# One pool of PSUM banks, a root on GpSimd, and other homes for VectorE's work in a two-layer kernel

## The chip, the cores and the metric

The kernel runs on one core of a Trainium2 chip. The metric is device time in microseconds (us), the median of several executions; one further execution was profiled. In the profile PE is TensorE, PEld its weight loads, DVE is VectorE, ACT is ScalarE, POOL is GpSimd and SP is SyncE, which issues most DMAs.

## The reference

Sixteen sequences of 512 tokens, each token 128 float32 values, go through two layers. Cut to what matters:

```python
# layer 0
xn = layernorm(x)
q, k, v = heads(xn @ Wq.T), heads(xn @ Wk.T), heads(xn @ Wv.T)     # 16 heads of 8
q, k = elu(rope(q)) + 1, elu(rope(k)) + 1
attn = causal linear attention (running sums of k v^T and of k, divided)
p = softmax(xn @ router.T); the best 2 of 8 experts per token, weights normalised
ffn = sum over the 2 experts of weight * relu(xn @ fc[e].T)**2 @ proj[e].T
      + relu(xn @ shared_fc.T)**2 @ shared_proj.T
x = x + attn @ Wo.T + ffn
# layer 1
xn = layernorm(x)
q, k, v = heads(xn @ W_qkv.T)
for each chunk of 64 queries: probs = softmax(q k^T / sqrt(8)) over the keys up to the chunk's end
    a gate from the sums of probs (two steps of a small dynamical system), rescale, probs @ v
xk = mu_k * xn + (1 - mu_k) * xn_previous;  xr likewise with mu_r
mix = sigmoid(xr @ W_r.T) * (relu(xk @ W_k.T)**2 @ W_v.T)
x = x + attn @ W_out.T + mix
```

## The kernel before

The work goes by sequence. A sequence's 512 tokens are four tiles (`NT`) of 128 partitions. Sequences are gathered in groups (`GROUPS`), since the experts need tokens of many sequences at once. For each group there are four chains of work. `dispatch` normalises the sequences (`layernorm_T`), finds the router's logits, routes (`route`, `places`) and scatters every token's row to two slots of a table in memory, by indirect DMAs on the POOL queue (`send`). `slot_tiles` runs over the table in tiles of 128 slots: it loads a tile's rows, turns them (`columns`), loads the weights of the tile's expert, and computes `hidden` (a product `hg_ps`, a rectifier on ACT, a square on DVE or POOL) and `project` (`yg_ps`). `layer0` runs the linear attention (`linear_operands`, `linear_attention`) and the `shared_expert`, whose last product `y` also takes in the attention's output. `layer1` runs, for each sequence, `head` (which gathers expert rows back by indirect DMAs and weighs them in `combine`, normalises, `channel_mix`, `values`, `projected`, `operands`), then `weighted` for each of two halves u of the heads, and then `tail` with `gated` and `gate_factor`.

A group with n token tiles needs a table of 2n + 7 slot tiles (`slot_count`), because each of eight experts may leave a tile part full.

Layer 1's attention works in two passes. `operands` builds padded queries `qa` and keys `ka`, multiplies them into scores (`sc`) and takes each row's maximum on DVE (`maxima`); after a transpose (`mx`) the maximum is taken off `qa`. `weighted` multiplies again with keys on the partitions (`st`), takes the exponential on ACT (`ex`), and multiplies by the padded values (`o`). Score products use 32 rows of the array at a time, products with values 32 columns, all others the full array: three forms of matmul. The linear attention has the same shape: scores with masked queries `q0m`, a causal product `am` on DVE, then `o`.

The order of instructions on each engine is not the order in which the code calls them. The class `Program` collects every operation with its needs and an assumed cost (`COSTS`, `TURN` for a change of matmul form, `HANDOVER` between engines), plays the program through in those costs, and emits each engine's instructions in the order found (`run`, `_take`, `_emit`); each engine then runs its queue strictly in that order. Hence almost every instruction of the profile carries one line (L261), that of the helper. Operations called inside `program.unit()` stay together. Indirect DMAs are kept at least `SPACE` apart in the plan, each placed behind a PE instruction.

The accumulators live in the eight PSUM banks. Two pools share them: `ps_big`, three tiles of two banks, and `ps_one`, two tiles of one bank.

```python
ps_big = pool("ps_big", 3, 24, space=bass.MemoryType.PSUM)
ps_one = pool("ps_one", 2, 24, space=bass.MemoryType.PSUM)
```

A tile comes free when its last reader (DVE or ACT) is done; a score unit of layer 1 asks for two tiles of `ps_big` at once.

Of the kernel before, what the change touches and what calls it, by code (L numbers as in the profile page):

```python
# [36 lines left out]
P = 128  # L37
# [9 lines left out]
GROUPS = (3, 4, 4, 3, 2)  # L47
FIRST = [sum(GROUPS[:g]) for g in range(len(GROUPS))]
GT = max(GROUPS) * NT
QUAD = 4  # L50

# [108 lines left out]
class Base:  # L160


    def __init__(self, slots, make):
        self.slots, self.make, self.tile = slots, make, None
        self.writers, self.readers = [], []
        self.left, self.free_at, self.users = 0, 0.0, []
# [7 lines left out]
class Slots:  # L174
# [3 lines left out]
    def __init__(self, n, ahead):  # L178
        self.free, self.asked, self.taken, self.waiting = [0.0] * n, [], 0, []
        self.ahead = ahead  # L180
# [19 lines left out]

class Op:
# [15 lines left out]
    ("ACT", None): (200, 0.8), ("POOL", None): (120, 1.75), ("SP", None): (80, 0.0),  # L217
}

# [7 lines left out]
class Program:  # L227
# [21 lines left out]
    def call(self, name, api, method, args, kw):  # L249
# [26 lines left out]
        else:  # L276
            form = method if (name, method) in COSTS else None
            if name == "DVE" and method in ("tensor_scalar", "tensor_scalar_min", "tensor_scalar_max"):
                form = "fast"
            if method in ("tensor_reduce", "bn_stats"):  # L280
                n = math.prod(args[1].shape[1:])
            least, each = COSTS[name, form]
            cost = least + each * n
            if kw.get("func", args[2] if len(args) > 2 else None) == AF.Sqrt:
                cost += 2600.0
# [46 lines left out]
    def run(self):  # L332
# [20 lines left out]
        while emitted < len(self.ops):  # L353
# [46 lines left out]
            for base in op.bases:  # L400
                base.left -= 1
                base.free_at = max(base.free_at, end + op.later)
                if not base.left:
                    heapq.heappush(base.slots.free, base.free_at + HANDOVER)
# [9 lines left out]
    def _take(self, op, start, offer):  # L414
# [6 lines left out]
        for bs in by_slots.values():  # L421
            slots = bs[0].slots
            if len(slots.free) < len(bs):
# [7 lines left out]
            ready = max(ready, heapq.nsmallest(len(bs), slots.free)[-1])  # L431
# [3 lines left out]
        for bs in by_slots.values():  # L435
            slots = bs[0].slots
            for b in bs:
                heapq.heappop(slots.free)
# [8 lines left out]
    def _passes(self, new):  # L447
# [9 lines left out]
        for bs in also.values():  # L457
            slots = next(iter(bs)).slots
            if len(slots.free) < len(bs):
# [29 lines left out]
def two_layers(ctx: ExitStack, tc: tile.TileContext, x, small, const, w_fc, w_proj, out):  # L489
# [19 lines left out]
    ps_big = pool("ps_big", 3, 24, space=bass.MemoryType.PSUM)  # L509
    ps_one = pool("ps_one", 2, 24, space=bass.MemoryType.PSUM)  # L510

    def big(name):
        return ps_big.tile([P, 2, 512], F32, tag="big", name=name)

    def one(name):
        return ps_one.tile([P, 512], F32, tag="one", name=name)
# [87 lines left out]
    eps = fixed.tile([P, 1], F32, tag="eps", name="eps")  # L604
    V.memset(eps, LN_EPS)
# [43 lines left out]
    def layernorm_T(xs, xT, name, tag, bufs):  # L649
# [7 lines left out]
        S.activation(rstd, mv[:, :, 1], AF.Sqrt, bias=eps, scale=1.0)  # L657
        V.reciprocal(rstd, rstd)
        xn = p2.tile([P, NT, D], F32, tag=tag, name=f"xn_{name}", bufs=bufs)
        for t in range(NT):  # L660
            V.tensor_scalar(
# [1047 lines left out]
```

## Time and profile before

| what | value |
|---|---|
| runs | 1669.26, 1670.35, 1676.13 us (median 1670.35) |
| profiled execution, its own time | 1665.29 us |
| its span, first to last instruction | 1663.5 us |
| mean granted TensorE clock | 0.973 |
| instructions | 36439 |
| DMA | 167.03 MB, mean 100 GB/s |
| matmul passes `hg_ps`, `yg_ps` | 1304 each, 182.5 and 188.5 us busy |
| `maxima` on DVE | 448 reductions, 385.8 us |
| `ex` on ACT | 320 exponentials, 313.1 us |

A float32 matmul is two passes, so a line of the profile counts two for one call. Busy shares are averages over a program whose stretches differ; the windows of the trace give them by stretch. A wait is booked to what ended it. A matmul that waits inside a row of its like is booked as busy, so the starts of consecutive rows tell more than the busy share. A row of the groups gives operation, output and inputs, shapes, count, busy time, mean length, and then the idle time before it with what ended it.

### The profile page before, as it was taken

What the parts mean: (1) busy time and instruction counts of PE and PEld (TensorE: products, weight loads), DVE (VectorE), ACT (ScalarE), POOL (GpSimd) and SP (SyncE); (2) the same over time, 40 slices, a digit from 0 to 9 for tenths busy, and PEclk for the clock granted to TensorE, in tenths of its full rate; (3) what the DMA queues carried; (4) which work ended last, traced back from release to release, by engine and by line L of the source; (5) the groups of instructions that cost most, each with busy time, mean ns of one, the idle gap of its engine ahead of it and who ended that gap; (6) DMA issues with size and microseconds to landing.
All of it is one profiled execution on the core that took longest, in us unless ns stands there. A gap on an engine that the chain in (4) does not pass through costs nothing.

```text
span 1663.5 us, 36439 instructions
## 1 busy us (share of the span) xinstructions
PE 1547.3 (93%) x14439; PEld 1021.8 (61%) x14439; DVE 1207.5 (73%) x2474; ACT 778.2 (47%) x1191; POOL 539.1 (32%) x485
## 2 busy tenths in 40 slices
PE   4889799999999999999999989999999999999996
PEld 3578776666766566566666656666565656565443
DVE  7875268877578874976758796968786858786773
ACT  4343334545445634444544655454545444535444
POOL 1415255075125421453033603242136202135020
PEclk8899999999999999999999999999999999999998
DMA  5367777144334423243322243324133313110000
GB/s 155 106 211 233 219 218 212 49 141 118 96 107 127 127 87 96 72 121 97 90 90 79 78 122 96 96 63 124 35 94 92 110 33 86 30 51 23 20 1 14
DMA packets 154986, 167.03 MB, mean 100 GB/s; under 512 B 13248, under 2 KB 100672, under 8 KB 154816
## 3 DMA queue, kind: packets, MB, share of 16 engines
q1 hardware_dynamic: 146624, 147.91, 29.9%
q0 software_dynamic: 8192, 16.79, 3.3%
q8 instruction: 114, 1.87, 0.5%
q14 instruction: 56, 0.46, 0.1%
HBM read 122.83 MB, written 41.81 MB: 99 GB/s over the span
## 4 chain that ended last, share of the span: by engine, by line
PE 53%; DVE 10%; issue 5%; ACT 3%; POOL 1%; DMA 0%; SPq 0%; POOLq 0%; ACTq 0%; DVEq 0%
PE o L261 10%; PE sc L261 10%; PE st L261 8%; PE yg_ps L261 5%; PE hg_ps L261 5%; DVE maxima L261 4%; PE y L261 3%; PE h_ps L261 2%; PE qkv L261 1%; PE qk L261 1%; PE ho_a L261 1%; ACT ex L261 1%; PE oh_a L261 1%; PE mx L261 1%; PE cm_r L261 1%
## 5 line engine op out<-in xcount | busy, mean ns | idle before, releaser
L261 DVE TENSOR_REDUCE maxima<-sc 128x2 f32<-128x768 f32 (+2 forms) x448 | 385.8, 912 | 84.6 <-PE sc L261 83.0
L261 ACT ACTIVATE ex<-st 128x1024 f32<-128x1024 f32 x320 | 313.1, 1025 | 177.5 <-PE st L261 176.3
L261 PE MATMUL st<-qa,ka 32*128 32x384 f32 (+3 forms) x2048 | 213.4, 471 | 9.6 <-DVE maxima L261 5.9
L261 PE MATMUL sc<-ka,qa 32*128 32x512 f32 (+2 forms) x1792 | 213.8, 511 | 3.7 <-DVE maxima L261 1.0
L1095 POOL DMA_INDIRECT rows<-xn,pl_slot x128 | 135.1, 1055 | 225.6 <-PE y L261 64.2
L261 PE MATMUL yg_ps<-wp,hg 128*128 128x128 f32 x1304 | 188.5, 287 | 17.5 <-DVE hg L261 9.4
L261 PEld LDWEIGHTS yg_ps<-wp,hg 128*128 128x128 f32 x1304 | 162.6, 195 | 66.9 <-issue 36.6
L1114 POOL DMA_INDIRECT back<-results,pl_slot x128 | 128.4, 1003 | 222.7 <-PE st L261 38.4
L261 PE MATMUL hg_ps<-xgT,wf 128*128 128x128 f32 x1304 | 182.5, 285 | 10.8 <-issue 6.3
L261 DVE TENSOR_TENSOR am<-sc,const_sb 128x1024 f32<-128x1024 f32 x128 | 151.3, 1218 | 53.7 <-PE sc L261 49.2
L261 PEld LDWEIGHTS hg_ps<-xgT,wf 128*128 128x128 f32 x1304 | 163.5, 196 | 35.9 <-issue 23.8
L261 PE MATMUL o<-ex,vpad 128*32 128x512 f32 (+3 forms) x2048 | 175.1, 447 | 1.7 <-ACT yg L261 1.3
L261 PEld LDWEIGHTS st<-qa,ka 32*128 32x128 f32 x2048 | 104.0, 186 | 81.4 <-issue 26.4
L261 ACT ACTIVATE hg<-hg_ps 128x1024 f32<-128x1024 f32 x84 | 84.2, 1002 | 135.7 <-PE hg_ps L261 135.3
L261 POOL TENSOR_TENSOR hg<-hg 128x1024 f32<-128x1024 f32 x34 | 64.6, 1901 | 224.1 <-ACT hg L261 223.9
L261 PEld LDWEIGHTS sc<-ka,qa 32*128 32x128 f32 x1792 | 90.5, 185 | 70.5 <-issue 25.8
L261 PEld LDWEIGHTS o<-ex,vpad 128*32 128x32 f32 x2048 | 52.2, 110 | 83.8 <-issue 59.5
L261 DVE TENSOR_TENSOR hg<-hg 128x1024 f32<-128x1024 f32 (+1 forms) x50 | 62.0, 1241 | 56.4 <-ACT hg L261 56.4
L261 ACT COPY oTs<-o 128x256 f32<-128x256 f32 (+1 forms) x96 | 42.7, 445 | 120.2 <-PE o L261 119.5
L261 ACT COPY yg<-yg_ps 128x256 f32<-128x256 f32 x84 | 30.9, 368 | 131.6 <-PE yg_ps L261 108.6
L261 PE MATMUL o<-am,vpad 128*32 128x128 f32 x2048 | 81.8, 281 | 8.7 <-DVE am L261 8.0
L261 PE MATMUL sc<-q0m,k0T 32*128 32x256 f32 x1024 | 81.3, 410 | 1.6 <-ACT ex L261 1.0
(193 smaller groups left out, 2289.1 us busy)
## 6 DMA issues: line engine op xcount, KB each, us to landing
wf<-in_w_fc SPq DMA_DIRECT2D x163, 256.0 KB
wp<-in_w_proj SPq DMA_DIRECT2D x163, 256.0 KB
results<-yg SPq DMA_DIRECT2D x79, 128.0 KB
xg<-rows SPq DMA_DIRECT2D x37, 256.0 KB
rows<-zeros SPq DMA_DIRECT2D x2, 2496.0 KB
x_in<-in_x SPq DMA_DIRECT2D x16, 256.0 KB
x<-x SPq DMA_DIRECT2D x16, 256.0 KB
out<-rr SPq DMA_DIRECT2D x16, 256.0 KB
```

The lines of the kernel that those rows point to most:

```text
L261: return getattr(api, method)(*map(made, args), **{k: made(a) for k, a in kw.items()})
L1095: i = nc.gpsimd.indirect_dma_start(out=rows.made()[:, :], out_offset=bass.IndirectOffsetOnAxis(ap=slot.made(), axis=0), in_=row.made(), in ...
L1114: "POOL", lambda: nc.gpsimd.indirect_dma_start(out=o.made(), out_offset=None, in_=results.made()[:, :], in_offset=bass.IndirectOffsetOnAxi ...
```

## The change

It has five parts.

1. Groups of 4, 4, 4 and 4 sequences in place of 3, 4, 4, 3 and 2. `LATE` is the first sequence of the last group.
2. One PSUM tile of eight banks. `Banks.place` chooses, for each operation that needs accumulators, which banks it takes (one, or two neighbours), and prefers not to leave single banks. The shared expert's and the experts' hidden products, and the two transposes of the linear attention, take one bank each and are emptied bank by bank.
3. No square root on ACT: the normaliser's root is a power on POOL, so ACT stays with one table of functions.
4. Work of DVE goes elsewhere: squares to ACT, most of `gate_factor` and the weighted sums of `combine` to POOL, the first step of `xr` and `xk` to ACT; for the last four sequences also the normalisation of layer 1, the operands of the first half and the gate's product to POOL. The masked queries `q0m` go from ACT to POOL.
5. The planner's costs for POOL and for DVE's per-partition scalars are new, its look-ahead over PSUM tiles is 48 instead of 24, and the expert products, the projection `yg_ps`, `y` and `qk` are units.

The diff, cut to its core:

```diff
-GROUPS = (3, 4, 4, 3, 2)
+GROUPS = (4, 4, 4, 4)
+LATE = B - GROUPS[-1]
...
+class Banks:
+    def __init__(self, pool, n, ahead):
+        self.pool, self.n, self.whole = pool, n, None
+        self.slots = Slots(n, ahead)
+        self.slots.free = [(0.0, k) for k in range(n)]
...
+    @staticmethod
+    def place(slots, bs, start):
+        free = {k: max(t, start) for t, k in slots.free}
+        best = None
+        def alone(k, rest):
+            return (k ^ 1) in rest
+        def fit(i, rest, at, ready, odd):
+            nonlocal best
+            if i == len(bs):
+                if best is None or ready + 400.0 * odd < best[0][0] + 400.0 * best[0][1]:
+                    best = ((ready, odd), list(at))
+                return
...
-    ("ACT", None): (200, 0.8), ("POOL", None): (120, 1.75), ("SP", None): (80, 0.0),
+    ("ACT", None): (200, 0.8), ("POOL", None): (240, 1.63), ("POOL", "fast"): (120, 1.14),
+    ("POOL", "each"): (60, 2.97), ("POOL", "memset"): (100, 0.84), ("SP", None): (80, 0.0),
...
-    ps_big = pool("ps_big", 3, 24, space=bass.MemoryType.PSUM)
-    ps_one = pool("ps_one", 2, 24, space=bass.MemoryType.PSUM)
+    banks = Banks(
+        ctx.enter_context(tc.tile_pool(name="psum", bufs=1, space=bass.MemoryType.PSUM)), 8, 48
+    )
...
-        S.activation(rstd, mv[:, :, 1], AF.Sqrt, bias=eps, scale=1.0)
-        V.reciprocal(rstd, rstd)
+        G.tensor_scalar_add(rstd, mv[:, :, 1], LN_EPS)
+        G.tensor_tensor(rstd, rstd, root, ALU.pow)
...
-            V.tensor_scalar(
+            (G if late else V).tensor_scalar(
                 xn[:, t, :], xs[:, t, :], mv[:, t, 0:1], rstd[:, t : t + 1], ALU.subtract, ALU.mult
...
-            for o in range(2):
-                r = 2 * u + o
-                S.activation(qm[:, o, :], pts[:, 0, :], AF.Copy, scale=c_("pick")[:, r : r + 1])
+            G.tensor_tensor(
+                qm, qT.unsqueeze(1).to_broadcast([P, 2, T]),
+                c_("pick")[:, 2 * u : 2 * u + 2].unsqueeze(2).to_broadcast([P, 2, T]), ALU.mult,
+            )
...
-            S.activation(hf, ph, AF.Relu)
-            (V if fp or b < GROUPS[0] else G).tensor_tensor(hf, hf, hf, ALU.mult)
+                ph = one(f"h_ps_{b}_{f}")
+                M.matmul(ph, wfc_s[:, f * P : (f + 1) * P], xnT, start=True, stop=True)
+                S.activation(hf[:, i, :], ph, AF.Relu)
+            if fp or b < GROUPS[0]:
+                S.activation(hf, hf, AF.Square)
+            else:
+                G.tensor_tensor(hf, hf, hf, ALU.mult)
...
-            ph = big(f"hg_ps_{g}_{q}_{pair}")
+                ph = one(f"hg_ps_{g}_{q}_{i}")
+                with program.unit():
...
+                S.activation(h[:, ii, :], ph, AF.Relu)
...
-            (V if pair or g == 0 else G).tensor_tensor(o, o, o, ALU.mult)
+            if pair or g == 0:
+                S.activation(o, o, AF.Square)
+            else:
+                G.tensor_tensor(o, o, o, ALU.mult)
...
-            for t in range(NT):
-                n = k * NT + t
-                V.scalar_tensor_tensor(
-                    x1[:, t, :], y[:, t, :], shares[j][:, n, :], x1[:, t, :],
-                    ALU.mult, ALU.add,
-                )
+            share = shares[j][:, k * NT : (k + 1) * NT, :]
+            G.tensor_tensor(y, y, share.to_broadcast([P, NT, D]), ALU.mult)
+            G.tensor_tensor(x1, x1, y, ALU.add)
...
+        A = G
...
-        V.tensor_mul(en, sums, rl)
-        V.tensor_scalar_max(sc, en, 1e-6)
+        A.tensor_mul(en, sums, rl)
+        A.tensor_scalar_max(sc, en, 1e-6)
...
+        if u == 0 and b < LATE:
+            V.scalar_tensor_tensor(
+                halves(qa), halves(q), own, spread("aug_q", u, 1), ALU.mult, ALU.add
+            )
...
+        else:
+            G.tensor_tensor(qa, q, own.to_broadcast([P, T]), ALU.mult)
+            G.tensor_tensor(halves(qa), halves(qa), spread("aug_q", u, 1), ALU.add)
...
-        V.tensor_tensor(ov, ov, fac.unsqueeze(2).to_broadcast([P, NT * H, DH]), ALU.mult)
+        (G if b >= LATE else V).tensor_tensor(ov, ov, fac.unsqueeze(2).to_broadcast([P, NT * H, DH]), ALU.mult)
...
-            V.tensor_scalar_mul(m, xp[:, 0:T], om)
+            S.activation(m, xp[:, 0:T], AF.Copy, scale=om)
```

In `gate_factor` the three reciprocals and the two `scalar_tensor_tensor` stay on DVE and the two tanh on ACT; all else is on POOL.

## The prediction

> **What bounds the kernel now.** I read the page first: busy shares, the slices, then the chain.
>
> ```profile
> PE 1547.3 (93%) x14439; PEld 1021.8 (61%) x14439; DVE 1207.5 (73%) x2474; ACT 778.2 (47%) x1191; POOL 539.1 (32%) x485
> ...
> PE   4889799999999999999999989999999999999996
> ...
> PEclk8899999999999999999999999999999999999998
> ...
> PE 53%; DVE 10%; issue 5%; ACT 3%; POOL 1%; DMA 0%; SPq 0%; POOLq 0%; ACTq 0%; DVEq 0%
> ```
>
> PE is the bound: 93% busy, and 53% of the chain that ended last. But the chain also gives DVE 10% (166 us), so a busy PE is not always a working PE. The timeline of PE shows it: start, length, form.
>
> ```profile
> 648.06 1.06 PE L261 MATMUL hg_ps<-xgT,wf 128*128 128x128 f32 x8
> 648.96 1.08 PE L261 MATMUL cm_k<-xk,small_sb 128*128 128x512 f32 x2
> ...
> 655.41 1.16 PE L261 MATMUL v<-small_sb,xp 128*128 128x128 f32 x8
> 656.49 1.07 PE L261 MATMUL o<-ex,vpad 128*32 128x384 f32 x16
> ...
> 1535.36 1.15 PE L261 MATMUL sc<-ka,qa 32*128 32x384 f32 x16
> 1536.43 1.09 PE L261 MATMUL ho_a<-const_sb,oTs 128*128 128x128 f32 x8
> 1537.46 6.30 PE L261 MATMUL sc<-ka,qa 32*128 32x384 f32 x32
> ```
>
> From start to start, eight expert passes behind their like take 0.90 us, eight passes of that form behind a 32-row stretch 1.08 (655.41 to 656.49), sixteen score passes 1.07. The 32 score passes at 1537.46 should take 2.15 us and are booked busy for 6.30: PE waited for banks that VectorE had not emptied (one `maxima` reduction of 1024 columns is 1.218 us). Spacing every matmul of the program as the undisturbed stretches do (0.22 us for a 128-wide product of full form, 0.11 for a transpose, 0.06 to 0.22 for a 32-row or 32-column one, plus 0.14 to 0.2 for a switch of form) gives an estimate of 1415 us of work in the 1663.5 us span. About 250 us are stalls, start-up, end and clock. The windows say where:
>
> ```profile
> 0.00:60.00 60.00, 33.54 (x210) 21.65 (x210) 45.64 (x163) 23.64 (x46) 14.86 (x31) 0.83 0.47 144
> 60.00:300.00 240.00, 216.18 (x1967) 175.74 (x1971) 158.06 (x352) 97.05 (x163) 101.36 (x90) 0.96 0.66 202
> 300.00:900.00 600.00, 579.75 (x5568) 388.32 (x5567) 446.91 (x875) 288.49 (x451) 202.98 (x175) 0.99 0.34 100
> 900.00:1500.00 600.00, 574.70 (x5452) 363.56 (x5448) 456.58 (x874) 293.43 (x437) 186.24 (x163) 0.99 0.27 79
> ...
> 1527.00:1646.00 119.00, 111.95 (x955) 54.59 (x953) 76.95 (x152) 54.94 (x70) 21.37 (x18) 0.96 0.03 10
> ...
> 1646.00:1663.50 17.50, 4.15 (x19) 3.24 (x19) 7.94 (x29) 1.94 (x5) 0.00 (x0) 0.62 0.05 15
> ```
>
> The first number after the length is PE busy, the third DVE, the fourth ACT, the fifth POOL. PE idles 26 us in the first 60; in the middle DVE is at 75%, POOL at 32%; the last 17.5 us are a chain of small gate operations with PE almost empty.
>
> **The change part by part.** My sum runs against the profiled execution, 1665.3 us; the median of the runs is 1670.35, 5 us above.
>
> *Seven tiles fewer.* A group of n token tiles reserves 2n+7 expert tiles: 163 over five groups, 156 over four. By the groups' rows a tile costs PE (182.5 + 188.5 + 27.1)/163 = 2.44 us: 17 us, all on PE.
>
> *Switches.* `program.unit()` keeps the passes of an expert tile, a projection or the shared output together. In the order of PE's instructions the changes of form fall from 1016 to 943: 73 x 0.15 = 11 us, less about 2 counted with the tiles: 9.
>
> With the same spacing the new program is 1389 us of PE work: 26 less, the same two terms.
>
> *Where the regions lie.* The last `y` product, after which PE has layer 1 alone, stands 65 us of work before the end in the old order and 145 us in the new, because the last group has four sequences, not two. In the trace it ends at 1562: 1350 us of work in 1562 (86%), then 62 in 84 (74%) up to 1646, then the 17.5 us end. At unchanged rates the new program takes 1244/0.864 = 1440, 141/0.74 = 190 and the end. So the long tail takes back about 14 us of the 26.
>
> *The end.* The gate moves 20 of its 25 instructions per sequence from DVE (7.9 us from first reciprocal to last product) to POOL. No row has POOL at 64 columns; from 1.07 us at 512 and 1.90 at 1024 a straight line gives 0.34, with DVE's 0.22 as the lower end and 0.7 (the 512-wide scalar form) as the upper. I take 0.34, since both rows lie on the line: with the hops between engines about 12 us, +4 (0 to +9). End 21.5. Subtotal: 1440 + 190 + 21.5 = 1651.
>
> *DVE relief.* Removed, by group rows: squares 62.0 + 23.0, weighted sums 45.1, gate 80.1, the first halves of `xr`,`xk` 17.1, the root's reciprocal 5.4, a quarter of `qa`,`ka` (39.1), of `xn` (27.2) and of `o1n` (11.1), 19: 252 us, leaving 955 (57 to 58%). One pool of banks also lets a one-bank product take any free bank, where two were set apart before, and the halves of an expert pair are emptied bank by bank. So DVE's part of the stalls should shrink. At unchanged rates 196 us of non-work lie before the tail and 49 in it; I take a fifth off the first (36: start-up and clock stay) and a quarter off the second (13: each late sequence has some 11 us less on DVE). 1651 - 49 = 1602. Bounds: nothing, and a half (-123).
>
> *Root tables.*
>
> ```profile
> L261 ACT ACT_TABLE_LOAD x48 | 61.6, 1283 | 21.2 <-PE st L261 19.2 <-PEq L1699 0.7 <-DVE phi L261 0.6
> ```
>
> One load is left of 48. The row prices one at 1.283 us, 60 in all; the Trainium skill, "ScalarE: Activation LUTs", What ACT_TABLE_LOAD costs, says about 2.7, which would make it 127. The row decides. Either way it is ACT's time and ACT is 47% busy: freed are 61.6 + 9.6 (roots) + 39.4 (`q0m`), and squares (about 70), split rectifiers (15) and `xr`,`xk` (20) come in, so ACT stays near 773 us. What hides it is ACT's slack; on the path only start-up (five loads in its first 30 us) shows it: a few us, inside the fifth above. POOL's power of four columns has no row; between 0.1 (a one-column memset) and 1.9 us (a 1024-wide product), I take 0.3, on the small side.
>
> *POOL.* It gains `q0m` (32 x 1.90 = 61), sums (64 x 1.07 = 68), gate (320 x 0.28 = 90), roots 13 and late parts 11; the operands cost 119 for 128 and ten squares less about -9: 539 becomes about 764, 46%. Each sum also holds the queue for its gather, about 1.7 us (gather issue ends 216.9, first use 218.5), 32 times: 54 us behind which gate and operands stand. Here a rule speaks against the change:
>
> ```profile
> L261 DVE SCALAR_TENSOR_TENSOR x<-back,rt_m,x x128: 318/344/2306, 218.5 to 1572.4; 128x128 f32<-128x128 f32 x128
> ...
> 572.70 2.33 DVE L261 TENSOR_SCALAR xn<-x,ln_mv,ln_rstd 128x128 f32<-128x128 f32 x2
> 573.03 1.92 POOL L261 TENSOR_TENSOR hg<-hg 128x1024 f32<-128x1024 f32 x1 [10.69 <-ACT hg L261]
> ```
>
> The same operation takes 344 ns in the median and 2306 at worst; the second pair shows why: `xn` ends as POOL's product ends. On average (404 ns by its group) this costs 17%, with POOL's tensor work at 16% of the span. That work rises to 29%: 30% of the 215 us of such DVE work that is left, about +30 us. The Trainium skill, "SBUF — State Buffer", Who interferes with whom, calls the shared port pair an exclusive lock, so the loser waits the whole instruction: some 550 such instructions x 29% x 0.5 us = 80. DVE ends at 985 or at 1035, both under 1207: the sum stands by the first, the range keeps the second.
>
> *Edits at nothing.* The causal product in another view, two routing tiles in others' storage, the two transposes in a bank each: same work, same engines. A unit makes others wait for its length (4.66 us for the 40 passes of `y`), but `y` stood nearly whole already (86 stretches, 64 now); if that cover is gone, 16 waits of a few us on ACT, not on PE. The planner's new prices and deeper look-ahead take no time; they reorder all, which is why the fifth above may be a half or nothing.
>
> *DMA and SP.* Seven tiles fewer are 14 weight loads of 256 KB; PE waited 3.2 us for weights in all: nothing, and if that cover is gone, still a gain.
>
> Sum 1602 on the profiled execution; 1607 with the 5 us, rounded to 1608.
>
> **The rivals.**
> *R1, only the arithmetic.* DVE relief frees no bank sooner because the order was already packed to these costs: 1651, 1656 measured. For it: PE shows only 50 us idle between 300 and 1600. Against it: the 6.30 us row, whose waits count as busy.
> *R2, DVE queues behind POOL (slower).* Four DVE instructions of each gate (reciprocals, `gf_z`, `gf_v`) and 28 normalisations now wait for POOL: about 100 waits, each ahead of `maxima` reductions in DVE's queue, which free PE's banks. POOL's queue itself waits for gathers and for the PE instruction behind which each gather is put. Before, DVE's waits of this sort (root from ACT) were 9.7 us over 32, 0.3 each: 30 us, hidden. It decides above 1656 + 100 x d = 1670, 0.15 us a wait that reaches PE with R1's relief, or 0.6 us with mine. At 1 us each with half the relief: 1632 + 100 = 1732, 1700 at 0.7.
> *R3, the stalls were mostly banks.* Half go: 1528 to 1560.
>
> **How the numbers follow.** Mine (1575 to 1645) 0.52, R1 (1645 to 1665) 0.16, R2 (over 1665) 0.18, R3 (under 1575) 0.14. About 0.5%, 8 us, can be told from no change, so faster is below 1662: 0.52 + 0.14 + most of R1 (0.12) = 0.78; same (1662 to 1679) 0.07; slower 0.15. The range 1550 to 1685 leaves a few in a hundred of R3 and a tenth of R2 outside.
>
> **What would show it.** Expert passes 1248 per group instead of 1304; DVE near 985 us, POOL near 764, ACT near 775 with one table load; DVE's share of the chain under 8%; score groups of 32 passes shorter than 6 us in the tail; last 20 us a POOL chain. If DVE's waits for POOL total over 60 us and PE's for DVE do not fall, R2 is right. If DVE is lighter and PE's start-to-start times stay, R1.

## The result, and the profile after

The kernel after takes 1749.05 us (median of four runs, 1741.76 to 1751.2), beside 1672.71 for the kernel before on the same chip. The ratio is 1.0449, with a 95% interval of 1.0408 to 1.0489: slower by about 75 us, where I had forecast 1608 us and a gain. The profiled execution took 1751.2 us, its span 1749.4.

The page of the kernel after: busy times, slices of PE, granted clock by slice, and the shares of the chain that ended last.

```profile
PE 1529.1 (87%) x14316; PEld 1008.2 (58%) x14316; DVE 995.6 (57%) x1803; ACT 774.0 (44%) x1247; POOL 807.3 (46%) x964
...
PE   5788988779899998999999989889998988878885
...
PEclk7789999899999999999999999999999989989898
...
PE 59%; POOL 14%; DVE 11%; issue 7%; DMA 5%; ACT 4%; POOLq 0%; SPq 0%; DVEq 0%; ACTq 0%
```

PE is 18 us less busy than before, in the direction that fewer tiles and fewer changes of form had promised; DVE is 212 us lighter. Yet PE idles 220 us, where it idled 116. In the chain POOL rose from 1% to 14% and DMA from nothing to 5%, although POOL is busy only 46% of the time: its busy share alone does not show this.

The windows of the kernel after, cut where its own stages lie: length, busy time of PE, PEld, DVE, ACT and POOL, then granted clock, DMA share and GB/s. The experts' products run from 136 to 1407 us, the last `y` product ends near 1527.

```profile
60.00:300.00 240.00, 210.55 (x2045) 173.77 (x2044) 97.61 (x213) 99.04 (x183) 90.03 (x84) 0.95 0.60 179
300.00:900.00 600.00, 542.68 (x5134) 361.63 (x5135) 383.15 (x727) 275.98 (x448) 311.93 (x353) 0.96 0.35 105
900.00:1400.00 500.00, 466.49 (x4512) 307.69 (x4513) 287.57 (x428) 234.95 (x379) 200.61 (x239) 0.97 0.28 83
1400.00:1527.00 127.00, 107.58 (x946) 63.69 (x947) 79.86 (x122) 49.31 (x77) 85.75 (x97) 0.91 0.08 24
1527.00:1749.40 222.40, 170.17 (x1596) 82.72 (x1592) 104.80 (x154) 97.55 (x125) 96.30 (x153) 0.89 0.04 11
```

Between 300 and 900 us PE is at 90%, where it was at 97%, with POOL at 52% for 34% and DVE at 64% for 74%. In the last 222 us PE is at 77%. The two kernels do not do the same work in the same stretch, since their groups differ; pool_undone below has this kernel's groups and shows where the time was lost.

The waits of the kernel after, all engines: who waited, for whose output; then us in total, times, and the longest.

```profile
POOL back L317 <- DMA back<-results,pl_slot: 59.5, 29, 4.6
...
DVE gf_z L317 <- POOL gf_z L317: 44.1, 19, 5.4
DVE ln_st L317 <- POOL x L317: 43.6, 11, 9.9
...
PE banks L317 <- DVE maxima L317: 38.2, 42, 4.1
...
DVE xn L317 <- POOL ln_rstd L317: 31.2, 13, 5.1
...
DVE gf_cur L317 <- POOL gf_sc L317: 20.8, 11, 7.2
...
DVE o1n L317 <- POOL gf_rl L317: 14.2, 9, 3.9
...
PE banks L317 <- POOL o1n L317: 11.3, 1, 11.3
...
DVE gf_v L317 <- POOL gf_z L317: 10.4, 11, 2.1
```

DVE's waits for POOL (these, and 1.9 us for `rr`) are 75 waits and 166 us, 2.2 us each. In the kernel before there were three, 8 us in all:

```profile
DVE rr L261 <- POOL hg L261: 6.7, 1, 6.7
DVE rr L261 <- POOL xp L261: 1.1, 1, 1.1
DVE rr L261 <- POOL rr L261: 0.3, 1, 0.3
```

Summed over all its waits, PE's idle time behind DVE rose from 74 to 117 us, behind ACT from 22 to 55, behind POOL from 0.5 to 37. Together that is 113 us more, of which 7 came back in its other waits. The idle time as a whole rose by 104 us; less the 18 by which PE is less busy, it is the 86 us by which the span grew.

The timeline of the kernel after shows what one such wait does: start, length, engine, operation, and in brackets the idle time before it with what ended it.

```profile
301.38 0.94 POOL L1193 DMA_INDIRECT back<-results,pl_slot  x1 [0.31 <-issue]
...
303.59 0.85 PE L317 MATMUL banks<-am,vpad 128*32 128x128 f32 x20
304.93 1.04 POOL L317 TENSOR_TENSOR back<-back,rt_m 128x512 f32<-128x512 f32 x1 [2.61 <-DMA back<-results,pl_slot]
306.05 1.26 POOL L317 TENSOR_TENSOR x<-x,back 128x512 f32<-128x512 f32 x1
307.34 0.29 DVE L317 BATCH_NORM_STATS2 ln_st<-x 128x6 f32<-128x128 f32 x1 [6.71 <-POOL x L317]
...
311.14 2.69 DVE L317 TENSOR_SCALAR xn<-x,ln_mv,ln_rstd 128x128 f32<-128x128 f32 x4 [0.36 <-POOL ln_rstd L317]
...
313.21 1.15 PE L317 MATMUL banks<-const_sb,xn 128*128 128x128 f32 x4 [8.78 <-DVE xn L317]
314.16 1.92 PE L317 MATMUL banks<-xgT,wf 128*128 128x128 f32 x8
...
318.06 0.94 POOL L1193 DMA_INDIRECT back<-results,pl_slot  x1 [2.49 <-PE banks L317]
...
320.68 1.03 POOL L317 TENSOR_TENSOR back<-back,rt_m 128x512 f32<-128x512 f32 x1 [1.68 <-DMA back<-results,pl_slot]
...
321.99 1.04 POOL L317 TENSOR_TENSOR ln_rstd<-ln_rstd,root 128x4 f32<-128x4 f32 x1
...
323.07 1.30 DVE L317 TENSOR_SCALAR xn<-x_in,ln_mv,ln_rstd 128x128 f32<-128x128 f32 x1 [5.07 <-POOL ln_rstd L317]
```

Follow it downwards. POOL issues a gather and then stands 2.61 us for its rows, because the sum is next in its queue. Product and sum take 2.3 us. DVE has the statistics of `x` next in its own queue and stands 6.71 us. PE has the transposes of the normalised rows next and stands 8.78 us: the wait reaches every engine, and each adds its own step to it. Some ten microseconds later the second kind appears. A root for another sequence (`x_in`, layer 0, nothing to do with the gather) lies in POOL's queue behind the gather, the wait for its rows and the product, and DVE stands 5.07 us for four numbers per partition.

### The profile page after: what moved, and what is told of

The parts are those of the page before. It is cut to its first block, busy times and chain, and to the rows that moved or that the text cites. A ratio compares the mean times of both kernels' runs of the same rounds, so it can differ in the third digit from the quotient of the medians.

```text
span 1749.4 us, 36128 instructions
## 1 busy us (share of the span) xinstructions
PE 1529.1 (87%) x14316; PEld 1008.2 (58%) x14316; DVE 995.6 (57%) x1803; ACT 774.0 (44%) x1247; POOL 807.3 (46%) x964
## 4 chain that ended last, share of the span: by engine, by line
PE 59%; POOL 14%; DVE 11%; issue 7%; DMA 5%; ACT 4%; POOLq 0%; SPq 0%; DVEq 0%; ACTq 0%
PE banks L317 59%; DMA back<-results,pl_slot 4%; DVE maxima L317 3%; POOL back L1193 3%; ACT ex L317 1%; POOL q0m L317 1%; POOL back L317 1%; POOL ka L317 1%; POOL ln_rstd L317 1%; POOL x L317 1%; DVE xn L317 1%; POOL hg L317 1%; DVE am L317 1%; ACT hg L317 1%; POOL gf_z L317 1%
## 5 line engine op out<-in xcount | busy, mean ns | idle before, releaser
L317 DVE TENSOR_REDUCE maxima<-banks 128x2 f32<-128x768 f32 (+2 forms) x448 | 384.7, 911 | 136.8 <-PE banks L317 123.1
L317 ACT ACTIVATE ex<-banks 128x1024 f32<-128x1024 f32 x320 | 310.8, 1022 | 157.6 <-PE banks L317 151.8
L317 PE MATMUL banks<-ka,qa 32*128 32x512 f32 (+2 forms) x1792 | 197.7, 526 | 44.6 <-DVE maxima L317 20.1
L317 DVE TENSOR_TENSOR am<-banks,const_sb 128x1024 f32<-128x1024 f32 x128 | 150.7, 1217 | 143.2 <-PE banks L317 133.2
L317 PE MATMUL banks<-qa,ka 32*128 32x512 f32 (+3 forms) x2048 | 197.2, 471 | 25.0 <-DVE maxima L317 12.6
L317 PE MATMUL banks<-ex,vpad 128*32 128x512 f32 (+3 forms) x2048 | 181.1, 455 | 2.7 <-DVE xs L317 1.7
L317 PE MATMUL banks<-xgT,wf 128*128 128x128 f32 x1248 | 174.9, 286 | 8.3 <-ACT hg L317 3.9
L317 PE MATMUL banks<-wp,hg 128*128 128x128 f32 x1248 | 162.1, 285 | 22.0 <-POOL hg L317 11.0
L317 PEld LDWEIGHTS banks<-xgT,wf 128*128 128x128 f32 x1248 | 156.5, 197 | 39.2 <-issue 16.3
L317 PEld LDWEIGHTS banks<-wp,hg 128*128 128x128 f32 x1248 | 152.6, 199 | 36.1 <-POOL hg L317 12.0
```

What stands on the lines that cost most here:

```text
L317: return getattr(api, method)(*map(made, args), **{k: made(a) for k, a in kw.items()})
```

## The experiments

Two bases are used. "The kernel after" has groups of four. `undone_old_groups` (1647 us) has the old groups and none of POOL's new work, and single parts are put onto it. The kernel before was measured beside every batch, each batch on another chip, and a ratio is to it. Its own median moved between 1667 and 1676 us from batch to batch, so differences between kernels are taken from the ratios; one per cent is 16.7 us.

| kernel | median us | ratio (interval) |
|---|---|---|
| after | 1749.05 | 1.0449 (1.0408 to 1.0489) |
| groups_as_before | 1731.72 | 1.0339 (1.0320 to 1.0358) |
| gate_on_dve | 1737.23 | 1.0358 (1.0337 to 1.0379) |
| root_on_act | 1709.12 | 1.0234 (1.0217 to 1.0251) |
| sums_on_dve | 1690.66 | 1.0080 (1.0061 to 1.0098) |
| sums_root_back | 1681.20 | 1.0087 (1.0062 to 1.0113) |
| pool_undone | 1666.44 | 0.9938 (0.9921 to 0.9954) |
| planner_told | 1722.20 | 1.0308 (1.0286 to 1.0330) |
| after_told | 1703.14 | 1.0213 (1.0178 to 1.0249) |
| before_fours | 1673.82 | 1.0019 (0.9999 to 1.0040) |
| undone_old_groups | 1647.22 | 0.9857 (0.9840 to 0.9873) |
| gate_alone | 1661.12 | 0.9940 (0.9916 to 0.9965) |
| root_alone | 1654.62 | 0.9901 (0.9867 to 0.9934) |
| sums_alone | 1692.20 | 1.0123 (1.0082 to 1.0163) |
| sums_landing | 1678.92 | 1.0058 (1.0031 to 1.0085) |
| sums_root_back_old_groups | 1683.36 | 1.0099 (1.0073 to 1.0124) |
| squares_on_dve | 1674.81 | 1.0030 (1.0008 to 1.0052) |
| old_pools | 1685.47 | 1.0091 (1.0062 to 1.0120) |
| two_pools | 2436.68 | 1.4601 (1.4559 to 1.4642) |

### Which part of the change it is

**groups_as_before.**

```diff
-GROUPS = (4, 4, 4, 4)
+GROUPS = (3, 4, 4, 3, 2)
```

> The kernel after, with groups of 3, 4, 4, 3 and 2 sequences again and all else kept. Three theories of the 77 us: P, POOL serves late (sums, gate, root and late operands wait in its queue, and VectorE and TensorE wait for them); G, four groups of four start the experts later (first expert product at 136 us for 100) and leave a longer layer-1-only end (219 us for 101); B, the one pool of banks with its new costs packs the order so tightly that every late operand stops TensorE. G: 1680 to 1700, since start (36 us) and end come back, less the 17 us of seven tiles more. P and B: 1740 to 1770, the tiles' 17 us added and little gained.

1731.72: 1.1% of the kernel's 4.5% came back. Groups of four cost something here, but three quarters of the loss stay.

**sums_on_dve.**

```diff
-            share = shares[j][:, k * NT : (k + 1) * NT, :]
-            G.tensor_tensor(y, y, share.to_broadcast([P, NT, D]), ALU.mult)
-            G.tensor_tensor(x1, x1, y, ALU.add)
+            for t in range(NT):
+                n = k * NT + t
+                V.scalar_tensor_tensor(
+                    x1[:, t, :], y[:, t, :], shares[j][:, n, :], x1[:, t, :],
+                    ALU.mult, ALU.add,
+                )
```

> The kernel after, with the weighted sums of the two expert rows on VectorE again (four fused products per gather, 45 us in all, for 64 products and sums of 512 columns, some 70 us, on POOL). P: 1715 to 1735, because POOL's queue no longer stands for the gathered rows (59.5 us of its waits in the kernel after) and the layer-1 statistics no longer wait for POOL's x (43.6 us of VectorE's waits). G and B: within 10 us of 1749.

1690.66: by the ratios 3.7%, 62 us less, more than P had asked for, with DVE 64 us busier (1059.9 for 995.6). Of the parts taken back one at a time this one gave the most: 76 us of products and sums left POOL (33.7 and 42.5).

**gate_on_dve.**

```diff
-        A = G
+        A = V
```

> The kernel after, with 20 of the gate's 25 instructions per sequence on VectorE again (about 80 us there, about 90 off POOL). P: 1715 to 1735, VectorE's waits for gf_z and gf_cur (65 us) gone, and ACT's for gf_v and gf_en (56). G and B: 1745 to 1770, since VectorE has 80 us more and nothing of theirs moves.

1737.23: 0.9%, 15 us back, just short of P's mark, and this with DVE 89 us busier. The gate's move costs, but it is not the main thing.

**pool_undone.** The two edits above, and:

```diff
-LATE = B - GROUPS[-1]
+LATE = B
...
-        G.tensor_scalar_add(rstd, mv[:, :, 1], LN_EPS)
-        G.tensor_tensor(rstd, rstd, root, ALU.pow)
+        S.activation(rstd, mv[:, :, 1], AF.Sqrt, bias=root[:, 0:1], scale=1.0)
+        V.reciprocal(rstd, rstd)
...
-            G.tensor_tensor(
-                qm, qT.unsqueeze(1).to_broadcast([P, 2, T]),
-                c_("pick")[:, 2 * u : 2 * u + 2].unsqueeze(2).to_broadcast([P, 2, T]), ALU.mult,
-            )
+            for o in range(2):
+                r = 2 * u + o
+                S.activation(qm[:, o, :], qT, AF.Copy, scale=c_("pick")[:, r : r + 1])
```

> The kernel after, with everything that went to POOL taken back: sums, gate, and late normalisations, operands and gate products on VectorE, the root on ACT with VectorE's reciprocal and the planner's surcharge for it, the masked queries on ACT. Groups of four, one pool of banks, squares on ACT and the new costs stay. P: 1650 to 1690, most of the 77 us back. G: 1725 to 1750, the start and the end still long. B: 1720 to 1760.

1666.44, ratio 0.9938: the whole loss and more came back, although ACT loads tables again (54 of 1.283 us). P holds: 5.1% of the kernel's time, 85 us, is the work that went to POOL. G and B, as the main cause, are out. Two of its windows, cut at its own last `y` product (1444 us):

```profile
300.00:900.00 600.00, 569.12 (x5470) 378.85 (x5471) 449.35 (x931) 347.18 (x547) 217.58 (x193) 0.99 0.37 108
1444.00:1664.30 220.30, 176.90 (x1605) 84.08 (x1604) 138.06 (x278) 103.42 (x131) 30.07 (x24) 0.89 0.04 11
```

Its end is as long as that of the kernel after (220 us for 222). The loss lies before: the last `y` product comes at 1444 us and not at 1527, which is 83 us. So the long end with PE at 77% belongs to the groups of four, and what POOL cost was paid ahead of it. PE's passes are the same in both, 14316. They are busy 1502.7 us here and 1529.1 in the kernel after, so some 26 of the 85 us stand in longer passes and 59 in idle time: PE's waits behind DVE are 88 us here for 117, behind POOL 3 for 37, and behind ACT 54 for 55. The rise behind ACT is therefore not POOL's doing.

### The root, and what the plan believed

**root_on_act.** Only the root's two lines of pool_undone, with the planner's surcharge of 2600 for a square root.

```diff
-        G.tensor_scalar_add(rstd, mv[:, :, 1], LN_EPS)
-        G.tensor_tensor(rstd, rstd, root, ALU.pow)
+        S.activation(rstd, mv[:, :, 1], AF.Sqrt, bias=root[:, 0:1], scale=1.0)
+        V.reciprocal(rstd, rstd)
```

> The kernel after, with only the root on ACT again (a square root, VectorE's reciprocal, the planner's surcharge for the table); sums, gate and late work stay on POOL. In the kernel after, VectorE's normalisations waited 31 us for ln_rstd, behind a sum that waited for its gathered rows, and a power took 1.045 us where the plan had 0.25. If the root's place in POOL's queue is a cause by itself: 1715 to 1735. If it only suffers from the sums: within 8 us of 1749, or up to 10 slower by the table loads that return (about 60 us of ACT's time, hidden).

1709.12: 2.2%, 36 us below the kernel after, beyond what I had set as the most. The row of the groups that I had had no value for:

```profile
L317 POOL TENSOR_TENSOR ln_rstd<-ln_rstd,root 128x4 f32<-128x4 f32 x32 | 33.4, 1045 | 2.7
```

A power of four columns takes 1.045 us, as long as a product of 512. The plan has it at 240 + 4 x 1.63 = 247 ns.

**planner_told.**

```diff
+            if name == "POOL" and ALU.pow in args:
+                cost = 1050.0
...
-            ), [results.base, slot.base], [o.base], 1260.0, 2000.0,
+            ), [results.base, slot.base], [o.base], 1260.0, 4000.0,
```

> The kernel after, with the same instructions on the same engines, but the plan told two durations: 1.05 us for POOL's power (0.25 planned) and 4.0 us from the issue of a gather to its rows (2.0 planned; POOL waited 2.0 us on average on top). If POOL's work is late only because the plan took it for early: 1690 to 1715, most of what sums_on_dve gained, since the sums stand later in the queue and the statistics with them. If the queue is the cause whatever the plan knows, because the gathers, sums and roots follow one another in one strict order and each gather stands behind a PE instruction: 1735 to 1755.

1722.20: 1.4%, 24 us less. Only the first edit had an effect: the planner sets the landing to 2000 for every transfer of POOL (`op.later = 2000.0`), whatever it was given. So this is the power's price alone, between my two expectations. DVE's waits for `ln_rstd` fell from 31.2 us:

```profile
DVE xn L317 <- POOL ln_rstd L317: 7.2, 7, 2.1
```

Presumably the plan now puts the normalisation later and something else in its place; this is not shown.

**sums_root_back.** The edits of sums_on_dve and of root_on_act together, on the kernel after.

```diff
+                V.scalar_tensor_tensor(
+                    x1[:, t, :], y[:, t, :], shares[j][:, n, :], x1[:, t, :],
...
+        S.activation(rstd, mv[:, :, 1], AF.Sqrt, bias=root[:, 0:1], scale=1.0)
+        V.reciprocal(rstd, rstd)
```

> The kernel after, groups of four kept, with both queue holders taken back: sums on VectorE, root on ACT. The gate, the masked queries and the late normalisations, operands and gate products stay on POOL. Alone the sums gave 58 us and the root 40, all of POOL's work 83. If the two only cost by each other (a root behind a sum that waits for its rows): 1680 to 1692, hardly below sums_on_dve. If each holds VectorE by itself: 1655 to 1670, at or below pool_undone (1666), with the gate and the rest on POOL costing nothing or helping. If the gate's waits (gf_z and gf_cur, some 50 us of VectorE's) reach TensorE too: 1672 to 1685.

1681.20, ratio 1.0087, for 1.0080 with the sums alone: taking the root back as well gave nothing that can be told from noise. So its 36 us came only together with the sums, which stood ahead of it in POOL's queue and waited for their rows. With the sums on DVE, its waits had already fallen, as the waits of sums_on_dve show:

```profile
DVE xn L317 <- POOL ln_rstd L317: 13.9, 13, 3.3
```

### The groups by themselves

**before_fours.** The kernel before with one line changed.

```diff
-GROUPS = (3, 4, 4, 3, 2)
+GROUPS = (4, 4, 4, 4)
```

> The kernel before, with groups of four groups of four and nothing else. My prediction's step on the regions gave seven tiles less (17 us) and a longer end (14 us back): 1665 to 1675. If groups of four cost by themselves: 1685 to 1705. A gain below 1660 would say that the long end is no loss.

1673.82, ratio 1.0019 (0.9999 to 1.0040): 3 us more, hardly clear of nothing, where my step on the regions made it 3 less. Seven tiles' gain and the longer end roughly cancel.

**undone_old_groups.** The edits of pool_undone and of groups_as_before together.

```diff
+GROUPS = (3, 4, 4, 3, 2)
...
+LATE = B
...
+        A = V
```

> pool_undone (1666) with groups of 3, 4, 4, 3 and 2 again: of the change there are left the one pool of banks, single-bank hidden products, units, squares and first steps on ACT, and the new costs. In the kernel after, the old groups gained 18 us. If groups of four cost by themselves (later experts, longer end): 1640 to 1655. If they cost only because their long end runs on POOL's late operands: 1665 to 1680, seven tiles (17 us) more, less a shorter start.

1647.22, ratio 0.9857: 24 us faster than the kernel before, the best kernel of this study. Beside pool_undone the old groups gain 0.8%, 13.5 us, and 18 beside the kernel after, but nothing in the kernel before. By the traces the part from the last `y` product on is 111 us shorter here than in pool_undone (109 for 220), and the part before it 97 longer. Between the kernel before and before_fours the same two figures are 116 and 103. Why the balance counts here and not there was not settled. Its page:

```profile
PE 1507.3 (91%) x14439; PEld 1001.8 (61%) x14439; DVE 1116.0 (68%) x2373; ACT 893.4 (54%) x1409; POOL 493.9 (30%) x453
...
PEclk9999999999999999999999999999999999999998
...
PE 69%; DVE 14%; ACT 8%; issue 5%; POOL 2%; DMA 2%; SPq 0%; POOLq 0%; DVEq 0%; ACTq 0%
```

DVE is 120 us busier than in the kernel after, and the program is 6% faster.

### Each part alone on the good base

**sums_alone, root_alone, gate_alone.** Each is undone_old_groups with one thing on POOL: in turn the sums, the root, the gate.

```diff
+            G.tensor_tensor(y, y, share.to_broadcast([P, NT, D]), ALU.mult)
+            G.tensor_tensor(x1, x1, y, ALU.add)
```

```diff
+        G.tensor_scalar_add(rstd, mv[:, :, 1], LN_EPS)
+        G.tensor_tensor(rstd, rstd, root, ALU.pow)
```

```diff
-        A = V
+        A = G
```

> undone_old_groups (1647) with one thing moved: the weighted sums on POOL. If holding the queue for the rows is harmful by itself, because the statistics of layer 1 wait on VectorE for x: 1670 to 1700. If it is harmful only through what stands behind it in POOL's queue (root, gate, masked queries): 1645 to 1660.

> undone_old_groups (1647) with one thing moved: the root is a power on POOL, planned at 0.25 us and lasting 1.05, and ACT loads one table instead of some fifty. If each normalisation's extra 0.8 us and its place in the queue cost by themselves: 1665 to 1685. If only behind the sums: 1640 to 1652, the tables' 60 us of ACT being a small gain.

> undone_old_groups (1647) with one thing moved: 20 of the gate's 25 instructions per sequence on POOL. Taken back from the whole, the gate gave 12 us; sums_root_back_old_groups (gate, masked queries and two late sequences on POOL) stands 36 above. If the gate's VectorE steps, each waiting for POOL, carry those 36: 1670 to 1685. If the gate is harmless where nothing else holds the queue, and the masked queries carry them: 1642 to 1655.

From 0.9857: the sums cost 2.7% (44 us), the gate 0.8% (14), the root 0.4% (7, and the intervals overlap a little). The sums are harmful by themselves. The root costs little when it stands behind no sum that waits for rows, though DVE waits 23.1 us for it. The gate's price is clear in its waits:

```profile
DVE gf_z L317 <- POOL gf_z L317: 44.5, 23, 4.4
...
DVE gf_v L317 <- POOL gf_z L317: 16.4, 13, 3.0
...
DVE o1n L317 <- POOL gf_rl L317: 11.6, 7, 3.3
...
DVE gf_cur L317 <- POOL gf_sc L317: 10.2, 13, 1.4
```

That is 83 us of waiting to take 78 us of work off DVE (1116.0 to 1038.1). The time of the engine was exchanged for time in which it stands, and the program is 14 us longer.

**sums_root_back_old_groups.** The edit of sums_root_back with the old groups.

```diff
-GROUPS = (4, 4, 4, 4)
+GROUPS = (3, 4, 4, 3, 2)
```

> The same with groups of 3, 4, 4, 3 and 2: beside undone_old_groups (1647) only the gate, the masked queries and the last two sequences' operands are on POOL. If VectorE's lighter load helps where no queue is held: 1630 to 1643. If each short POOL step in a chain costs its wait: 1650 to 1665.

1683.36, above both expectations: 1.6%, 27 us more than gate_alone, from the masked queries and the last two sequences' operands, normalisation and gate product. These were not told apart. The single prices (44, 14 and 7) and these do not add to the whole exactly: all of POOL's work on the old groups costs 80 us (1.0339 for 0.9857).

**sums_landing.** The planner adds a transfer's landing only for a consumer on another engine. POOL issues the gathers and now also uses them, so a sum was planned with no landing at all.

```diff
-                seen = end + (op.later if other.engine != name or name == "SP" else 0.0)
+                seen = end + (op.later if other.engine != name or name == "SP" or op.spaced else 0.0)
...
```

> sums_alone (1692), same instructions on the same engines, but the plan counts the 2.0 us of a gather's landing for POOL's own sums too. If the sums are late only because the plan had them start at the last gather's issue: 1650 to 1670, with POOL's waits for its gathered rows well under the 68 us of sums_alone. If sums on POOL cost by themselves (one strict queue with gathers that each stand behind a PE instruction, x a step later): 1680 to 1700.

1678.92, between the two: about 11 us less than sums_alone by the ratios, whose intervals overlap a little. The waits of sums_alone, then those of sums_landing:

```profile
POOL back L317 <- DMA back<-results,pl_slot: 68.0, 31, 3.6
...
DVE ln_st L317 <- POOL x L317: 39.3, 8, 9.9
```

```profile
DVE ln_st L317 <- POOL x L317: 21.1, 5, 6.8
...
POOL back L317 <- DMA back<-results,pl_slot: 19.4, 14, 4.6
```

POOL's wait for the rows fell by 49 us, the time by 11. Most of the sums' price, some 34 us, is not the missing landing. What it is was not isolated: DVE still waits for `x` 21 us, and the product and sum of 2.3 us come between the rows and the statistics.

**after_told.** The kernel after with both prices put right.

```diff
+            if name == "POOL" and ALU.pow in args:
+                cost = 1050.0
...
-                seen = end + (op.later if other.engine != name or name == "SP" else 0.0)
+                seen = end + (op.later if other.engine != name or name == "SP" or op.spaced else 0.0)
```

> The kernel after, same instructions on the same engines, with both prices put right in the plan: 1.05 us for the power, and the 2.0 us of landing for POOL's own sums. The power's price alone gave 27 us (1722). If the wrong prices are most of the loss: 1675 to 1700. If the landing adds little: 1710 to 1725.

1703.14: by the ratios 39 us less than the kernel after, with the same instructions on the same engines, of which the power made 24. So of the 85 us of POOL's work not quite half was an order planned on these two wrong times. The other 46 stay, although POOL now hardly stands for its rows (59.5 us before the edit), since DVE still waits for POOL's results, 114 us in all:

```profile
DVE gf_z L317 <- POOL gf_z L317: 47.2, 21, 5.2
...
DVE ln_st L317 <- POOL x L317: 27.1, 7, 11.4
...
POOL back L317 <- DMA back<-results,pl_slot: 6.9, 9, 2.4
```

POOL's standstill for the gathers is thus a part of the price and not the whole of it.

### VectorE's relief, and the banks

**squares_on_dve.**

```diff
-                S.activation(hf, hf, AF.Square)
+                V.tensor_tensor(hf, hf, hf, ALU.mult)
...
-                S.activation(o, o, AF.Square)
+                V.tensor_tensor(o, o, o, ALU.mult)
```

> undone_old_groups (1647) with the squares on VectorE again (about 85 us of it; ACT is lighter by 70). If its gain of 24 us over the kernel before is VectorE's relief, as my prediction took it: 1660 to 1672. If it is the one pool of banks, the units and the costs: 1642 to 1655.

1674.81: 1.7%, 29 us, for 81 us of DVE (1197.2 for 1116.0). So with the one pool of banks a microsecond of squares off DVE is worth 0.36 us.

**old_pools.**

```diff
-    banks = Banks(
-        ctx.enter_context(tc.tile_pool(name="psum", bufs=1, space=bass.MemoryType.PSUM)), 8, 48
-    )
+    ps_big = pool("ps_big", 3, 24, space=bass.MemoryType.PSUM)
+    ps_one = pool("ps_one", 2, 24, space=bass.MemoryType.PSUM)
...
-                ph = one(f"hg_ps_{g}_{q}_{i}")
+            ph = big(f"hg_ps_{g}_{q}_{pair}")
...
```

> undone_old_groups (1647) with the banks as in the kernel before: three pairs and two singles under their own pools, a look-ahead of 24, hidden products and the two transposes in pairs. Units, costs, squares and first steps on ACT stay. If the one pool gives a part of the 24 us over the kernel before: 1655 to 1670. If it gives nothing and the lighter VectorE all: 1640 to 1650.

1685.47, above what I had allowed: 2.3%, 39 us, for the one pool with its longer look-ahead and bank-by-bank emptying. Without the one pool (1.0091 here), or without the squares' move (1.0030 in squares_on_dve), the kernel is no faster than the kernel before; with both it is. In old_pools DVE is 95 us lighter than in the kernel before (1112.0 for 1207.5) and the program is still 0.9% longer, so relief alone did not pay. The units, the new costs and ACT's added work (871 us for 778) were never taken back by themselves, and what they cost is open.

**two_pools.**

```diff
+    pairs = Banks(
+        ctx.enter_context(tc.tile_pool(name="ps_big", bufs=1, space=bass.MemoryType.PSUM)), 6, 48
+    )
     banks = Banks(
-        ctx.enter_context(tc.tile_pool(name="psum", bufs=1, space=bass.MemoryType.PSUM)), 8, 48
+        ctx.enter_context(tc.tile_pool(name="ps_one", bufs=1, space=bass.MemoryType.PSUM)), 2, 48
     )
...
-                ph = one(f"hg_ps_{g}_{q}_{i}")
+            ph = big(f"hg_ps_{g}_{q}_{pair}")
...
```

> undone_old_groups (1647) with the banks in two pools again, six for the pairs and two for the single ones, and the hidden products and the two transposes in pairs; units, costs, look-ahead and squares on ACT stay. If the gain over the kernel before comes from the one pool and from emptying bank by bank: 1660 to 1680. If from VectorE's relief and the units: 1642 to 1655.

2436.68, and it says nothing on the question. Its waits hold a kind that hardly occurs in the others, ACT's exponentials standing for VectorE's reductions of other accumulators (3.7 us in the kernel after):

```profile
ACT ex L317 <- DVE maxima L317: 88.6, 14, 15.1
```

Why was not settled; old_pools answers the question in its stead.

## Why the prediction was wrong

Its counts of work held in the main; its account of waiting failed. The result lies 141 us above the forecast of 1608, and an estimate from the runs splits that into three: 85 us that POOL's work cost (pool_undone); about 29 that the DVE relief through POOL was to bring (the 150 of the 252 us that pool_undone has on DVE again, at 0.19); and some 26 that are missing in pool_undone too. There DVE is 102 us lighter and the regions and switches stand, so the sum has 36 us less than the kernel before, and 10 came. Those 26 no run assigns; the open cost of units, planner's prices and ACT's added work is where they may lie.

- **Seven tiles fewer** and **Switches** (26 us of PE work less): PE is 18 us less busy, and 45 less in pool_undone, where it waits less. The direction held; a busy time is no measure of 26 us of work.
- **Where the regions lie** (gain of 17, loss of 14): 3 us slower alone in before_fours. Held to a few us. (The 14 taken back are of time: 26 us of work are 30 us at 86%, and 1440 + 190 for 1562 + 84 is 16 less.) In the kernel after, the region up to the last `y` ran 1244/1527 = 81% full, not 86%, and the end took 222 us, not 211. pool_undone has the same long end, so only the first of these rates was changed by POOL's waits.
- **The end:** I made the gate's chain 12 us with 0.34 us for a POOL operation of 64 columns. They take 0.24 to 0.44, and the last gate runs from 1730.61 to 1741.4, 10.8 us. Held.
- **Root tables:** one load is left and ACT is at 774.0 us (773 predicted). That a load's price is hidden held in root_alone and pool_undone: with some fifty loads back the program was no slower. The power was the mistake, 1.045 us for 0.3, in the middle of my bounds (0.1 to 1.9). As work that is 24 us on POOL. As an error in the order of the plan it cost 24 us of time, and I had not asked what the plan takes it for. My two prices of a load are no rivals: the Trainium skill, "ScalarE: Activation LUTs", What ACT_TABLE_LOAD costs, gives the load alone at about 1283 ns, as the row has it, and its total counts a drain besides.
- **DVE relief** (252 us off, 49 gained, 0.19 per us): the step assumed that an engine with less work releases sooner. Where the work goes to an engine that DVE doesn't wait for, and one pool of banks is there, this is right and was too small: the squares gave 0.36 per us. Where DVE itself waits for the moved work, it is wrong in sign: 78 us of gate off DVE made the program 14 us longer, the sums' move 44.
- **POOL, the step that failed.** It wrote down that a sum holds the queue for its gather, 54 us, "behind which gate and operands stand", and then put nothing for it in the sum: the paragraph goes on to contention, and 1602 is 1651 - 49 with no term for POOL. The hold measured 59.5 us, so the row was read well. The price of waiting for POOL, DVE's 166 us and through them PE's, was left at zero, and the sum even counted a gain for work whose result DVE waits for. All of POOL's part cost 85 us (pool_undone): 24 by the power's wrong price in the plan, about 16 by the missing landing (after_told), and 46 that stay when POOL hardly stands for its rows. POOL's own work was put too low as well, 764 us for 807: the roots take 42 us for 13, the gate 102 for 90 (the sum took 0.28 us an operation, where the line beside it gave 0.34), the sums 76 for 68.
- **Contention** (+30 us of DVE by the row, +80 as an estimate by the rule of the Trainium skill, "SBUF — State Buffer", Who interferes with whom): DVE ended at 995.6, nearer the 985 of the row than the 1035 of that estimate. `xn` of `x_in` takes 473 ns for 388, but `xk` 924 for 965. The row was the better guide, and it was the wrong question; how much of DVE's time was contention no run separates.
- **Rival R2** described what happened and gave 1700 to 1732. Its test was met: DVE's waits for POOL total 166 us, and PE's for DVE rose. I had 100 waits of up to 1 us; there were 75 of 2.2. By 85/75, an estimate that books all of POOL's price on these waits, some 1.1 us of each reached the end, far over the 0.6 from which R2 was to decide. It had a chance of 0.18, since the nearest row (DVE's waits for ACT's root, 0.3 us each) was taken for the size. ACT's queue, 47% busy, held no gathers. The range ended at 1685.
- **What would show it:** 1248 expert passes, and in the end no row of 32 score passes (16 at most, 2.09 us). Both came. DVE's share of the chain did not fall below 8% but is 11%.

## What to carry to other kernels

Before work is moved off a busy engine, ask whether that engine, or the next one in the chain, will wait for the result. If it will, price the wait, with all that stands before it in the other queue: transfers above all. Here the engine that issued the gathers and used their rows stood before 29 of its 32 products, and the strict queues handed each standstill on, with each engine's own step added: POOL 2.6, DVE 6.7, PE 8.8 us in one place. Even with that standstill planned away and the power's price right, more than half of the cost stayed. And where an order is planned from assumed times, each new kind of instruction is a new price to be measured, and each new pair of producer and consumer a rule to be read again: two wrong ones were worth 39 us here.

## What the runs showed of the hardware

A power on POOL takes 1.045 us for 4 columns, where its tensor products take 0.32 for 64 and 1.05 for 512. So four columns of this operation cost what 512 of another do.

After a standstill PE's passes were slow. The eight expert passes after the gap of 8.78 us took 1.92 us; eight of the same form took 1.06 before it, at 302.60. The windows of the kernel after around the gap show the granted clock, the third figure from the end:

```profile
300.00:304.00 4.00, 4.00 (x47) 3.72 (x47) 0.64 (x1) 1.28 (x3) 1.89 (x2) 1.00 0.52 154
304.40:313.20 8.80, 0.04 (x2) 0.02 (x1) 5.22 (x19) 0.37 (x1) 7.61 (x8) 0.74 0.46 137
313.20:318.00 4.80, 4.79 (x21) 4.55 (x22) 4.44 (x16) 2.11 (x4) 2.13 (x2) 0.50 0.23 62
```

The clock was full before the gap and half for 4.8 us after it. The Trainium skill, "TensorE: Matmul & The Clock Gate", The HAM clock gate, has the clock at half rate after idleness; this trace agrees, with 0.50. The mean granted clock of a run goes down with its idle time (0.941 in the kernel after, 0.955 in groups_as_before, 0.970 in pool_undone, 0.978 in undone_old_groups), but it counts the idle stretches too. Counted in windows of 1 us, PE was busy 167 us at a clock under 0.9 in the kernel after and 90 in pool_undone; its busy time multiplied by what the clock lacked is 76 and 42 us. By this estimate, and by the 26 us of longer passes above, about a third of the 85 us of POOL's price is this echo of the waits. No run separates the two by itself.
